# A transformer's selected tokens: moved by rank through a table in memory, in place of one-hot products on TensorE

## The chip, the cores and the metric

The kernel runs on one core of a Trainium2 chip. The metric is the device time of one execution in microseconds (us); the time before is the median of three runs. A profile is one further execution, recorded by the hardware profiler.

The engines are named as in the profile: PE (TensorE, matrix products; PEld is its loading of weights), DVE (VectorE), ACT (ScalarE), POOL (GpSimd) and SP (SyncE, which only issues transfers here). Each engine works through its own instructions in a fixed order and waits at an instruction until the semaphores it needs have come. Transfers between the memories (DMAs) are issued by SP, ACT or POOL and carried out by 16 DMA engines, which all three share.

## The reference

A Fourier neural operator turns 64 images of 256 x 256 into 256 rows of 256 numbers each; 77 rows of text are joined to them, which makes 333 tokens per sample. Then comes one transformer layer. What matters here is its second half, in which only 165 of the 333 tokens are processed:

```python
def ffn(x, wr, br, w1, b1, w2, b2):          # x: normalized tokens, (64, 333, 256)
    weights = (x @ wr + br)[..., 0]          # one weight per token
    k = 333 // 2                             # 166
    _, idx = top_k(weights, k)
    sel_idx = idx[:, :k - 1]                 # the 165 tokens of largest weight
    sel = take_along_axis(x, sel_idx[:, :, None], axis=1)
    h = gelu(sel @ w1 + b1)                  # 256 -> 1024
    y = h @ w2 + b2                          # 1024 -> 256
    y = y * take_along_axis(weights, sel_idx, axis=1)[..., None]
    processed = zeros_like(x).at[batch_idx, sel_idx].set(y)
    return processed + x

h = concatenate([fno(x), txt], axis=1)
h = h + attention(layernorm(h))
h = h + ffn(layernorm(h))
```

## The kernel before

The first 9,800 us, about, compute the Fourier operator over all 64 samples; nothing of that is touched. The last stage, here called the transformer stage, handles one sample after another. A sample's tokens lie in a tile of 128 partitions by three blocks of 256 numbers: two blocks of 128 image rows and one of 77 text rows (`rows = [128, 128, 77]`).

The stage's functions are these. `image_rows(b)` loads sample `b`'s field in eight pieces of 1 MB, `ch`, on SP's queue and contracts them on PE (L896) into the image rows `h`. `attention(h)` normalizes (`layer_norm`, name "a"), forms the attention's products on PE, has POOL add the output bias to `h` (L1020), and on DVE adds the attended values to that (L1027), which gives `h1`; a second `layer_norm` (name "f") gives `z`, the tokens of the feed-forward part.

`select(z)` computes each token's weight as a column (L940), spreads it over all partitions with a diagonal matrix `dg` (L944) and a product with ones (L945), and counts for every token on DVE how many tokens have a larger weight: `gt` (L958 to L963) is the token's rank from 0 to 332. `fw` is the weight where the rank is below KEPT = 165 and zero elsewhere (L964). `place` (L965) is a one-hot matrix of tokens by ranks, made by comparing the rank with a row of numbers from a table, `iota`.

`feed_forward(b, ...)` multiplies `z` by `place` on PE (L1042), which yields the selected tokens already transposed, `zs`; transposes `place` on PE into `back` (L1053); runs the two layers (L1059, L1070), each over 165 columns; transposes the result into `ys` (L1080), ranks on partitions; multiplies it by `back` (L1089), which puts every rank's row at its token and zeros elsewhere; and finally multiplies by `fw` and adds `h1 + z` on DVE (L1092, with the sum from POOL, L1085). Seventeen DMAs from POOL's queue store the sample's rows (L1097, L1101). `evict` copies a result from PE's accumulators (PSUM), on DVE and ACT in turn.

The main loop interleaves samples: it emits the image rows of sample b + 2, the attention of b + 1, the feed-forward of b, and the selection for b + 1. No order is written out by hand in this stage: a scheduler orders each engine's instructions, and a pool's number of buffers (`bufs`, two for most tiles here, six for PSUM) bounds how far samples may overlap. DMAs issued by POOL use eight semaphores in turn, so a DMA waits for the eighth before it to have landed.

Of the kernel before, what the change touches and what calls it, by code (L numbers as in the profile page):

```python
# [8 lines left out]

F32 = mybir.dt.float32  # L10
AF = mybir.ActivationFunctionType
ALU = mybir.AluOpType
AX = mybir.AxisListType
# [9 lines left out]
TOK = S + TXT  # L23
# [11 lines left out]
def _tables():  # L35

    y = np.arange(S)
    ky = np.arange(M)
    kx = np.concatenate([np.arange(M), np.arange(-M, 0)])
    th = 2 * np.pi * np.outer(y, ky) / S  # L40
    tx = 2 * np.pi * np.outer(y, kx) / S
    grid = np.linspace(0.0, 1.0, S, dtype=np.float32)
    p = np.arange(128)
    out = {}

    def halves(a):
        return a.reshape(2, 128, -1).transpose(1, 0, 2)

    def ravel(*dims):

        return np.unravel_index(np.arange(np.prod(dims)), dims)


    fy = np.zeros((S, 32))
    fy[:, :M], fy[:, M:KX] = np.cos(th), -np.sin(th)
    out["fyt"] = np.tile(fy.reshape(8, 32, 32).transpose(1, 0, 2), (4, 1, 1))
    ex = np.zeros((128, S))
    ex[:KX], ex[KX:2 * KX] = np.cos(tx).T, np.sin(tx).T
# [36 lines left out]
    m6 = np.zeros((128, 3, 2, 4, C))  # L95
    for g in range(3):
        for r in range(2):
            for k4 in range(4):
                m6[M * r + 4 * g + k4 + 32 * np.arange(4), g, r, k4] = 1
    out["m6"] = m6  # L100
    out["mk4"] = p[:, None] % 4 == np.arange(128)[None, :] // C

    g = grid.astype(np.float64)
    one = np.ones(S)
    gh = np.zeros((128, 3, 2, KX))
    for j, (a, b) in enumerate(((g, one), (one, g), (one, one))):
        m = np.outer(np.exp(-1j * tx).T @ a, np.exp(-1j * th).T @ b)
        for k4 in range(4):
            gh[4 * j + k4] = np.stack([m.real, m.imag])[:, :, k4::4].transpose(2, 0, 1)
    out["gh"] = gh  # L110

    t, g, n, hc = ravel(2, 4, 4, 8)
    x_of = 64 * n + 16 * g + 2 * hc + t
    out["exT"] = ex[:, x_of]
    out["mask4"] = p[:, None] // C == np.arange(4)[None, :]
    tok = np.concatenate([x_of, S + np.arange(TXT)])
    rows = np.stack([x_of[:128], x_of[128:], S + p], 1)
    out["iota"] = np.repeat(np.arange(KEPT)[None, :], 128, 0)
    out["tri"] = tok[None, None, :] < rows[:, :, None]
    out = {k: np.ascontiguousarray(v.reshape(128, -1), np.float32) for k, v in out.items()}  # L120

    mv = np.zeros((4, 32, 16, S), np.float32)
    mv[:, :KX] = t32[None, :KX, None, :]
    mv[:, 28] = grid
    return out, mv.reshape(128, 16 * S)
# [10 lines left out]
def tile_fno_fusion_transformer(ctx: ExitStack, tc: tile.TileContext, a, cst_d, grid_d, out):  # L136
    nc = tc.nc
# [640 lines left out]
    tcon = ctx.enter_context(tc.tile_pool(name="tcon", bufs=1))  # L778
    inp = ctx.enter_context(tc.tile_pool(name="inp", bufs=7))
    tabt = tables(tcon, "exT", "tri", "cstt")  # L780
    EXT, MASK4, IOTA = tabt("exT"), tabt("mask4"), tabt("iota")
    TRI = tabt("tri").rearrange("p (t j) -> p t j", t=3)
    qrow = tcon.tile([128, C, 1], F32, name="qrow")
    nc.vector.tensor_mul(qrow[:, :, 0], qR, s_)
# [12 lines left out]
    D = S  # L797
# [70 lines left out]
    pb_ = ctx.enter_context(tc.tile_pool(name="tpb", bufs=2, space=PSUM))  # L868
    pp = ctx.enter_context(tc.tile_pool(name="tpp", bufs=6, space=PSUM))

    def psum():
        return pp.tile([128, 512], F32, name="pp")

    def image_rows(b):
        am = ap_.tile([2 * KX, 32 * C], F32, name="am")
# [53 lines left out]
            evict(zT[:, dh, :], ps[:, :TOK], 2)  # L929
        return z, zT  # L930

    def select(z):


        wcol = small.tile([128, 3], F32, name="wcol")
# [10 lines left out]
        wrow = tp.tile([128, TOK], F32, name="wrow")  # L946
        nc.vector.tensor_scalar(wrow, ps[:, :TOK], brB, None, ALU.add)
        fw = small.tile([128, 3], F32, name="fw")
        place = tp.tile([128, 3, KEPT], F32, name="place")
        for t in range(3):  # L950
            r = rows[t]
            junk = tp.tile([128, TOK], F32, name="junk", bufs=1)
            wc = small.tile([128, 1], F32, name="wc")
            nc.vector.scalar_tensor_tensor(
                junk[:r, :r], wrow[:r, toks[t]], 1.0, ID[:r, :r], ALU.mult, ALU.mult, accum_out=wc[:r]
            )
            gt = small.tile([128, 1], F32, name="gt")
            nc.vector.tensor_scalar(junk[:r], wrow[:r], wc[:r], None, ALU.is_gt, ALU.add, accum_out=gt[:r])  # L958
            eq = small.tile([128, 1], F32, name="eq")
            nc.vector.scalar_tensor_tensor(  # L960
                junk[:r], wrow[:r], wc[:r], TRI[:r, t, :], ALU.is_equal, ALU.mult, accum_out=eq[:r]
            )
            nc.vector.tensor_add(gt[:r], gt[:r], eq[:r])  # L963
            nc.vector.tensor_scalar(fw[:r, t:t + 1], gt[:r], float(KEPT), wc[:r], ALU.is_lt, ALU.mult)  # L964
            nc.vector.tensor_scalar(place[:r, t, :], IOTA[:r], gt[:r], None, ALU.is_equal)  # L965
        return fw, place

    def attention(h):
        z, zT = layer_norm(h, "a")
# [41 lines left out]
        for jt in range(3):  # L1011
# [2 lines left out]
            for t in range(3):  # L1014
                nc.tensor.transpose(ps[:r, toks[t]], p_[:rows[t], t, toks[jt]], ID[:rows[t], :rows[t]])
            evict(pT[:r, jt, :], ps[:r, :TOK], 2)
        h1 = tp.tile([128, 3, D], F32, name="h1")
        for t in range(3):
            r = rows[t]
            nc.gpsimd.tensor_add(h[:r, t, :], h[:r, t, :], boB[:r])  # L1020
# [9 lines left out]
        z = layer_norm(h1, "f")  # L1030
        return h1, z

    kept = [slice(0, (KEPT + 1) // 2), slice((KEPT + 1) // 2, KEPT)]

    def feed_forward(b, h1, z, fw, place):

        zs = tp.tile([128, 2, KEPT], F32, name="zs")
        for dh in range(2):
            ps = psum()
            for t in range(3):  # L1040
                r = rows[t]
                nc.tensor.matmul(  # L1042
                    ps[:, :KEPT], lhsT=z[:r, t, 128 * dh:128 * dh + 128], rhs=place[:r, t, :],
                    start=t == 0, stop=t == 2,
                )
            evict(zs[:, dh, :], ps[:, :KEPT], 2)
        back = tp.tile([128, 2, TOK], F32, name="back")
        for c, k in enumerate(kept):
            n = k.stop - k.start
            ps = psum()  # L1050
            for t in range(3):
                r = rows[t]
                nc.tensor.transpose(ps[:n, toks[t]], place[:r, t, k], ID[:r, :r])  # L1053
            evict(back[:n, c, :], ps[:n, :TOK], 2)
        g = tp.tile([128, HID // 128, KEPT], F32, name="g", bufs=1)
        for hb in range(HID // 128):
            ps = psum()
# [18 lines left out]
        for c, k in enumerate(kept):  # L1076
            n = k.stop - k.start
            ps = psum()
            for dh in range(2):
                nc.tensor.transpose(ps[:n, 128 * dh:128 * dh + 128], yT[:, dh, k], ID)  # L1080
            evict(ys[:n, c, :], ps[:n, :D], 2)
        o = tp.tile([128, 3, D], F32, name="o")
        for t in range(3):
            r = rows[t]
            nc.gpsimd.tensor_add(h1[:r, t, :], h1[:r, t, :], z[:r, t, :])  # L1085
            ps = psum()
            for c, k in enumerate(kept):
                n = k.stop - k.start
                nc.tensor.matmul(  # L1089
                    ps[:r, :D], lhsT=back[:n, c, toks[t]], rhs=ys[:n, c, :], start=c == 0, stop=c == 1  # L1090
                )
            nc.vector.scalar_tensor_tensor(  # L1092
                o[:r, t, :], ps[:r, :D], fw[:r, t:t + 1], h1[:r, t, :], ALU.mult, ALU.add
            )
        for g in range(4):
            for n in range(4):
# [5 lines left out]

    hs = {n: image_rows(n) for n in range(min(2, B))}
    done = attention(hs.pop(0))
    done += select(done[1])
    for b in range(B):
        now = done
        if b + 2 < B:
            hs[b + 2] = image_rows(b + 2)
        if b + 1 < B:  # L1110
            done = attention(hs.pop(b + 1))
        feed_forward(b, *now)
        if b + 1 < B:
            done += select(done[1])


# [31 lines left out]
```

## Time and profile before

| | us |
|---|---|
| median of 3 runs | 12,356.92 (12,355.53 to 12,375.24) |
| the profiled execution's own time | 12,360.58 |
| its span, first to last instruction | 12,358.8 |
| from 10,000 to 12,000 us: samples in it | 50 |
| L1059 and L1070 (feed-forward products) in these 2,000 us, PE busy | 234.8 and 231.0 |
| L896 (image rows), PE busy | 364.1 |
| L1042, L1053, L1089 (one-hot products), PE busy | 92.7, 37.0, 143.4 |
| L1097 (output stores), POOL busy | 394.0 |

The page gives each engine's busy share in 40 slices of 309 us; a digit is a tenth, 9 stands for 90% and more, and PEclk is the clock that PE was granted. The view of groups gives busy time by line, operation and shape. The view of windows adds up each engine's busy time in a stretch. The timeline lists an engine's instructions in order of time, with the idle time before one in brackets and what ended it. A landing time is the time from a DMA's issue until its data are reported complete.

### The profile page before, as it was taken

Reading aid. Unit: us, or ns where it says so; the run is one execution under the profiler, and the core shown is the slowest. Engines: PE = TensorE matmul, PEld = TensorE weight load, DVE = VectorE, ACT = ScalarE, POOL = GpSimd, SP = SyncE. Lnnn points to the kernel's source line nnn. Section 1 sums busy time; section 2 is a strip of 40 time slices with the busy share of each in tenths; the row PEclk is TensorE's granted clock in tenths of the full one; section 3 lists DMA queues with packets and bytes.
Section 4 is the critical chain, followed back from the end, with each engine's and each line's share of the span. In section 5 each row is a group of like instructions: output and inputs, shape, how many; then the busy total and the mean of one; then the engine's idle time right before and its main releaser. Section 6 shows DMA issues by size and latency. Waiting matters only on the chain. (4 is left out here: it accounts for less than half of the span.)

```text
span 12358.8 us, 405064 instructions
## 1 busy us (share of the span) xinstructions
PE 11164.5 (90%) x182038; PEld 5874.0 (48%) x182038; DVE 8774.8 (71%) x10667; ACT 6094.5 (49%) x10249; POOL 1412.7 (11%) x1987
## 2 busy tenths in 40 slices
PE   6999999998799999999979999999999699999999
PEld 3444444443444444444434444444444366666666
DVE  6777777777776777777766777767777566666665
ACT  5555555555555555555544555555555333333333
POOL 0000000000000000000010000000000133333333
PEclk8999999999899999999989999999999799999999
DMA  7555555555899999888889989889899755555554
GB/s 226 200 199 203 203 201 201 201 200 210 325 354 349 349 351 350 348 347 348 346 302 352 354 346 355 339 339 353 346 351 352 247 234 227 219 228 233 218 223 152
DMA packets 589283, 3485.06 MB, mean 282 GB/s; under 512 B 95000, under 2 KB 144536, under 8 KB 188568
## 3 DMA queue, kind: packets, MB, share of 16 engines
q1 hardware_dynamic: 539520, 3392.84, 71.2%
q0 software_dynamic: 40880, 62.59, 2.0%
q8 instruction: 1423, 23.31, 0.8%
q10 hardware_dynamic: 7144, 3.72, 0.1%
q14 instruction: 316, 2.59, 0.1%
HBM read 1761.87 MB, written 1696.92 MB: 280 GB/s over the span
## 5 line engine op out<-in xcount | busy, mean ns | idle before, releaser
L666 ACT ACTIVATE ring<-ring 128x1024 f32<-128x1024 f32 x3072 | 3108.8, 1012 | 1186.4 <-PE ring L659 1148.7
L647 DVE STREAM_TRANSPOSE t<-vo 128x2048 f32<-128x2048 f32 x1536 | 3550.0, 2311 | 175.1 <-ACT vo L642 14.5
L659 PE MATMUL ring<-vo,w 32*32 32x512 f32 x49152 | 2849.3, 622 | 392.2 <-DVE zt L686 138.7
L642 ACT ACTIVATE vo<-ring 128x1024 f32<-128x1024 f32 x1536 | 1568.2, 1021 | 2997.7 <-PE ring L635 2378.9
L643 DVE TENSOR_SCALAR vo<-ring 128x1024 f32<-128x1024 f32 x1536 | 1857.7, 1209 | 608.2 <-PE ring L635 420.4
L676 PE MATMUL ring<-t,cst 32*32 32x512 f32 x49152 | 1864.7, 601 | 303.7 <-issue 302.1
L686 DVE STREAM_TRANSPOSE zt<-ring 128x1024 f32<-128x1024 f32 x384 | 711.8, 1925 | 1658.6 <-PE ring L676 1658.6
L659 PEld LDWEIGHTS ring<-vo,w 32*32 32x32 f32 x49152 | 761.3, 105 | 1898.7 <-ACT ring L666 477.0
L676 PEld LDWEIGHTS ring<-t,cst 32*32 32x32 f32 x49152 | 975.9, 103 | 1157.0 <-issue 707.8
L594 POOL TENSOR_TENSOR ams<-am,sk 48x512 f32<-48x512 f32 x384 | 486.9, 1268 | 8642.4 <-DMA am<-mix 8039.9
L635 PE MATMUL ring<-vin,ws 32*32 32x512 f32 x32768 | 1238.0, 606 | 22.1 <-issue 19.8
L699 PEld LDWEIGHTS ring<-cst,zt 128*128 128x128 f32 x4608 | 536.4, 194 | 174.6 <-ACT vo L642 161.6
L666 ACT ACTIVATION_READ_ACCUMULATOR ring<-ring 128x1 f32 x3072 | 584.1, 190 | 0.0
L1097 POOL DMA_DIRECT2D out_dram<-o x1024 | 504.4, 501 | 659.8 <-DVE o L1092 628.2
L699 PE MATMUL ring<-cst,zt 128*128 128x96 f32 x4608 | 568.7, 281 | 8.1 <-DVE zt L686 8.1
L896 PE MATMUL hp<-ch,win 128*32 128x512 f32 x4096 | 472.0, 601 | 8.3 <-DMA ch<-v 8.1
L635 PEld LDWEIGHTS ring<-vin,ws 32*32 32x32 f32 x32768 | 253.5, 103 | 407.9 <-issue 377.8
L605 PE MATMUL ring<-ams,cst 49*128 49x512 f32 (+1 forms) x1536 | 391.5, 621 | 37.6 <-POOL ams L594 27.2
L901 ACT ACTIVATE h<-hp,hbias 128x512 f32<-128x512 f32 x64 | 44.0, 687 | 595.5 <-PE hp L896 595.5
L419 PE MATMUL mps<-wm,xh 32*64 32x128 f32 (+1 forms) x4608 | 121.3, 374 | 203.4 <-ACT e L431 74.1
L1059 PE MATMUL pp<-zs,w 128*128 128x165 f32 x2048 | 302.1, 305 | 0.0
L1070 PE MATMUL pp<-g,w 128*128 128x165 f32 x2048 | 298.6, 303 | 0.0
(936 smaller groups left out, 11812.8 us busy)
## 6 DMA issues: line engine op xcount, KB each, us to landing
v<-vo SPq DMA_DIRECT2D x1536, 1024.0 KB
vin<-v SPq DMA_DIRECT2D x1024, 1024.0 KB
ch<-v SPq DMA_DIRECT2D x512, 1024.0 KB
mix<-ob SPq DMA_DIRECT2D x96, 512.0 KB
am<-mix SPq DMA_DIRECT2D x384, 96.0 KB
xin<-in_x_dram SPq DMA_DIRECT2D x16, 1024.0 KB
mv<-in_x_dram SPq DMA_DIRECT2D x256, 64.0 KB
out_dram<-o POOLq DMA_DIRECT2D x1024, 16.0 KB, 3.0
```

The source lines that it names most:

```text
L594: nc.gpsimd.tensor_tensor(ams[b % 2][hv], a_[hv], sk[hv].rearrange("p c k -> p (c k)"), ALU.mult)
L635: nc.tensor.matmul(ps[n][32 * j:32 * j + 32], lhsT=ws[32 * n:32 * n + 32], rhs=v[32 * n:32 * n + 32, 2 * j:2 * j + 2, :], start=False, sto ...
L642: nc.scalar.activation(of[:, 0:2], t2[0], AF.Relu)
L643: nc.vector.tensor_scalar(of[:, 2:4], t2[1], 0.0, None, ALU.max)
L647: nc.vector.transpose(t32[b, t // 2][:, :, 8 * (t % 2):8 * (t % 2) + 8, :].rearrange("p y s c -> p s y c"), o.rearrange("p s (y l) -> p s ...
L659: nc.tensor.matmul(ps[n][32 * j:32 * j + 32], lhsT=w4[i + 1][32 * n:32 * n + 32], rhs=o[32 * n:32 * n + 32, 2 * j:2 * j + 2, :], start=Tru ...
L666: nc.scalar.activation(t2[n], t2[n], AF.Square, accum_out=acc[:, at:at + 1])
L676: nc.tensor.matmul(ps[n][32 * j:32 * j + 32], lhsT=FYT[32 * n:32 * n + 32, k, :], rhs=t32[b, j][32 * n:32 * n + 32, k].rearrange("p s c -> ...
L686: nc.vector.transpose(zt[:, h].rearrange("p k c -> p c k"), t2[h].rearrange("p n (s c) -> p c (n s)", c=C),)
L699: nc.tensor.matmul(ps[:, 0, 96 * g:96 * g + 96], lhsT=zt[:, h, k0:k0 + 4, :].rearrange("p k c -> p (k c)"), rhs=FX[:, h, 48 * r:48 * r + 9 ...
L896: nc.tensor.matmul(hp[32 * g:32 * g + 32], lhsT=win[:, 7 - t:39 - t], rhs=ch[:, g], start=False, stop=t == 7, skip_group_check=True,)
L1097: nc.gpsimd.dma_start(out[b, 64 * n + 16 * g:64 * n + 16 * g + 16].rearrange("(p t) d -> p t d", t=2), o[32 * g + 8 * n:32 * g + 8 * n + 8 ...
```

## The change

The rank, until now compared with a row of numbers to make a one-hot matrix, is turned into an index. In `select`, each block of tokens is written by an indirect DMA, row by row, to its rank's row in a table in the chip's memory (`z_d`, 333 rows of 256 numbers; the name of the tile is `zr` with a number), and the first 165 rows are read back as `zr`, in two DMAs of 83 and 82 rows. In `feed_forward`, four transposes on PE turn `zr` into `zs`. The result `ys` is written to a second table (`y_d`, 166 rows, the last one zero, written once at the start), and an indirect DMA reads for every token the row of its rank, or the zero row where its rank is 165 or more (`idx[..., 1]`, the minimum of rank and 165). The last multiply-add and the stores move to a function `finish`, emitted one iteration later than before, after the next attention. There are three tables of either kind, used in turn, `h1` has three buffers in place of two, and the table `iota` goes.

```diff
+    z_d = [dram.tile([TOK, D], F32, name=f"zr{n}") for n in range(3)]
+    y_d = [dram.tile([KEPT + 1, D], F32, name=f"yr{n}") for n in range(3)]
+    zero = tcon.tile([1, D], F32, name="zero")
+    nc.vector.memset(zero, 0.0)
+    for q in y_d:
+        nc.gpsimd.dma_start(q[KEPT:KEPT + 1], zero)
...
-    def select(z):
+    def select(b, z):
...
-        place = tp.tile([128, 3, KEPT], F32, name="place")
+        idx = small.tile([128, 3, 2], U32, name="idx")
...
-            nc.vector.tensor_scalar(place[:r, t, :], IOTA[:r], gt[:r], None, ALU.is_equal)
-        return fw, place
+            nc.vector.tensor_copy(idx[:r, t, 0:1], gt[:r])
+            nc.vector.tensor_scalar(idx[:r, t, 1:2], gt[:r], float(KEPT), None, ALU.min)
+            nc.gpsimd.indirect_dma_start(
+                z_d[b % 3][:, :], bass.IndirectOffsetOnAxis(ap=idx[:r, t, 0:1], axis=0), z[:r, t, :], None
+            )
+        zr = tp.tile([128, 2, D], F32, name="zr")
+        for c, k in enumerate(kept):
+            nc.gpsimd.dma_start(zr[:k.stop - k.start, c, :], z_d[b % 3][k])
+        return fw, idx, zr
...
-        h1 = tp.tile([128, 3, D], F32, name="h1")
+        h1 = tp.tile([128, 3, D], F32, name="h1", bufs=3)
...
-    def feed_forward(b, h1, z, fw, place):
+    def feed_forward(b, h1, z, fw, idx, zr):
 
         zs = tp.tile([128, 2, KEPT], F32, name="zs")
-        for dh in range(2):
-            ps = psum()
-            for t in range(3):
-                r = rows[t]
-                nc.tensor.matmul(
-                    ps[:, :KEPT], lhsT=z[:r, t, 128 * dh:128 * dh + 128], rhs=place[:r, t, :],
-                    start=t == 0, stop=t == 2,
-                )
-            evict(zs[:, dh, :], ps[:, :KEPT], 2)
-        back = tp.tile([128, 2, TOK], F32, name="back")
+        ps = psum()
         for c, k in enumerate(kept):
             n = k.stop - k.start
-            ps = psum()
-            for t in range(3):
-                r = rows[t]
-                nc.tensor.transpose(ps[:n, toks[t]], place[:r, t, k], ID[:r, :r])
-            evict(back[:n, c, :], ps[:n, :TOK], 2)
+            for dh in range(2):
+                nc.tensor.transpose(
+                    ps[:, KEPT * dh + k.start:KEPT * dh + k.stop], zr[:n, c, 128 * dh:128 * dh + 128], ID[:n, :n]
+                )
+        evict(zs.rearrange("p h k -> p (h k)"), ps[:, :2 * KEPT], 2)
...
+        for c, k in enumerate(kept):
+            nc.gpsimd.dma_start(y_d[b % 3][k], ys[:k.stop - k.start, c, :])
         o = tp.tile([128, 3, D], F32, name="o")
         for t in range(3):
             r = rows[t]
+            nc.gpsimd.indirect_dma_start(
+                o[:r, t, :], None, y_d[b % 3][:, :], bass.IndirectOffsetOnAxis(ap=idx[:r, t, 1:2], axis=0)
+            )
             nc.gpsimd.tensor_add(h1[:r, t, :], h1[:r, t, :], z[:r, t, :])
-            ps = psum()
-            for c, k in enumerate(kept):
-                n = k.stop - k.start
-                nc.tensor.matmul(
-                    ps[:r, :D], lhsT=back[:n, c, toks[t]], rhs=ys[:n, c, :], start=c == 0, stop=c == 1
-                )
+        return o, h1, fw
+
+    def finish(b, o, h1, fw):
+        for t in range(3):
+            r = rows[t]
             nc.vector.scalar_tensor_tensor(
-                o[:r, t, :], ps[:r, :D], fw[:r, t:t + 1], h1[:r, t, :], ALU.mult, ALU.add
+                o[:r, t, :], o[:r, t, :], fw[:r, t:t + 1], h1[:r, t, :], ALU.mult, ALU.add
             )
...
     done = attention(hs.pop(0))
-    done += select(done[1])
+    done += select(0, done[1])
+    last = None
     for b in range(B):
         now = done
         if b + 2 < B:
             hs[b + 2] = image_rows(b + 2)
         if b + 1 < B:
             done = attention(hs.pop(b + 1))
-        feed_forward(b, *now)
+        if last:
+            finish(b - 1, *last)
+        last = feed_forward(b, *now)
         if b + 1 < B:
-            done += select(done[1])
+            done += select(b + 1, done[1])
+    finish(B - 1, *last)
```

More of the change, by code (lines that the diff above doesn't have):

```diff
@@ L10 @@
 F32 = mybir.dt.float32
+U32 = mybir.dt.uint32
 AF = mybir.ActivationFunctionType
@@ L117, in _tables @@
     rows = np.stack([x_of[:128], x_of[128:], S + p], 1)
-    out["iota"] = np.repeat(np.arange(KEPT)[None, :], 128, 0)
     out["tri"] = tok[None, None, :] < rows[:, :, None]
@@ L780, in tile_fno_fusion_transformer @@
     tabt = tables(tcon, "exT", "tri", "cstt")
-    EXT, MASK4, IOTA = tabt("exT"), tabt("mask4"), tabt("iota")
+    EXT, MASK4 = tabt("exT"), tabt("mask4")
     TRI = tabt("tri").rearrange("p (t j) -> p t j", t=3)
@@ L869, in tile_fno_fusion_transformer @@
     pp = ctx.enter_context(tc.tile_pool(name="tpp", bufs=6, space=PSUM))
+    kept = [slice(0, (KEPT + 1) // 2), slice((KEPT + 1) // 2, KEPT)]
     def psum():
         return pp.tile([128, 512], F32, name="pp")
+    z_d = [dram.tile([TOK, D], F32, name=f"zr{n}") for n in range(3)]
[4 more added lines that the diff above has]
+        nc.gpsimd.dma_start(q[KEPT:KEPT + 1], zero)
     def image_rows(b):
@@ L1031, in attention @@
         return h1, z
-    kept = [slice(0, (KEPT + 1) // 2), slice((KEPT + 1) // 2, KEPT)]
-    def feed_forward(b, h1, z, fw, place):
+    def feed_forward(b, h1, z, fw, idx, zr):
         zs = tp.tile([128, 2, KEPT], F32, name="zs")
-        for dh in range(2):
-            ps = psum()
-            for t in range(3):
-                r = rows[t]
-                nc.tensor.matmul(
-                    ps[:, :KEPT], lhsT=z[:r, t, 128 * dh:128 * dh + 128], rhs=place[:r, t, :],
-                    start=t == 0, stop=t == 2,
-                )
-            evict(zs[:, dh, :], ps[:, :KEPT], 2)
-        back = tp.tile([128, 2, TOK], F32, name="back")
+        ps = psum()
         for c, k in enumerate(kept):
             n = k.stop - k.start
-            ps = psum()
-            for t in range(3):
-                r = rows[t]
-                nc.tensor.transpose(ps[:n, toks[t]], place[:r, t, k], ID[:r, :r])
-            evict(back[:n, c, :], ps[:n, :TOK], 2)
+            for dh in range(2):
[3 more added lines that the diff above has]
+        evict(zs.rearrange("p h k -> p (h k)"), ps[:, :2 * KEPT], 2)
         g = tp.tile([128, HID // 128, KEPT], F32, name="g", bufs=1)
```

## The prediction, written before the changed kernel ran

> **What bounds the kernel now.** I read the page's slices first, to find the stage that the change touches, then a table of windows over one period of it, then the timeline of each engine over the same period, then the landing times of POOL's DMAs. The change lies in the transformer stage alone: the last eight slices of the page (from about 9,800 us), in which each of 64 samples is one period.
>
> ```profile
> PE   6999999998799999999979999999999699999999
> DVE  6777777777776777777766777767777566666665
> POOL 0000000000000000000010000000000133333333
> PEclk8999999999899999999989999999999799999999
> ```
>
> ```profile
> core 0: us, PE busy (x) PEld busy (x) DVE busy (x) ACT busy (x) POOL busy (x), PEclk, DMA share, GB/s
> 11005.00:11009.00 4.00, 4.00 (x30) 2.31 (x32) 3.50 (x6) 0.44 (x1) 3.85 (x8) 1.00 0.15 25
> 11009.00:11031.00 22.00, 21.81 (x132) 12.66 (x122) 17.64 (x75) 8.55 (x16) 6.71 (x13) 1.00 0.98 392
> 11031.00:11042.00 11.00, 10.56 (x76) 10.04 (x75) 4.79 (x15) 5.97 (x15) 2.52 (x3) 1.00 0.08 27
> ```
>
> PE is busy for 39.1 of the 40.0 us of a period (the four windows from 11,002 to 11,042 summed), at full clock: PE bounds the stage. To be seen as well: the DMA engines are full (0.98) for 22 us of each period, while the eight 1 MB loads `ch` of a later sample run, and nearly idle for the other 18.
>
> ```profile
> 11001.41 0.45 PE L1080 MATMUL pp<-cst,yT 128*83 128x128 f32 x2 [0.27 <-ACT yT L1074]
> 11002.26 2.87 PE L1089 MATMUL pp<-ys,back 83*128 83x256 f32 x12 [0.41 <-DVE ys L178]
> 11004.97 0.61 PE L945 MATMUL pp<-dg,cst 128*128 128x128 f32 x4
> ...
> 11029.43 1.85 PE L1042 MATMUL pp<-place,fz 128*128 128x165 f32 x12
> 11031.12 0.74 PE L1053 MATMUL pp<-cst,place 128*83 128x128 f32 x6
> 11031.70 4.70 PE L1059 MATMUL pp<-zs,w 128*128 128x165 f32 x32
> ```
>
> The columns are start, length, engine, line. L1080 recurs at 11,041.38: a period is 40.0 us. L1042 and L1053 fill 11,029.43 to 11,031.70; L1089 and the wait before it fill 11,001.86 to 11,004.97.
>
> ```profile
> 11005.15 7.86 POOL L1097 DMA_DIRECT2D out_dram<-o  x16 [9.83 <-DVE o L1092]
> 11013.00 0.53 POOL L1101 DMA_DIRECT2D out_dram<-o  x1
> 11021.70 2.18 POOL L1020 TENSOR_TENSOR h<-h,boB 128x256 f32<-128x256 f32 x3 [8.17 <-DVE az L918]
> 11032.78 2.52 POOL L1085 TENSOR_TENSOR h<-h,fz 128x256 f32<-128x256 f32 x3 [8.90 <-DVE fz L918]
> ```
>
> POOL works 13.1 us of 40 and waits for data the rest; nothing on PE waits for it today. The landing times of its stores, from the view of one line in a window: 1.7 to 1.8 us for the first two L1097 after 11,005 (DMA engines nearly idle), 1.8 us median in the last 18 us of the kernel (no loads left), but a median of 3.1 us and up to 8.0 us for L1097 over 10,000 to 12,000 us, and 5.3 to 8.6 us for L1101, the last of each 17.
>
> **What the Trainium skill says.** "DMA: Bandwidth & Descriptors", section "Anatomy of one DMA", puts the fixed cost of a GpSimd DMA at about 2.0 us; the trace agrees where the engines are idle (1.7 to 1.8). Its section "Queues, rings and completion order" says that a DMA engine takes turns between queues a packet at a time; so under the `ch` load every small packet waits for a large one, which fits the 3 to 8 us. Its section "Two DMAs through the same engine are not ordered" says that a DMA that reads what another wrote must wait for that one's completion; the changed kernel's program has these waits. No page prices the issue of an indirect DMA.
>
> **The change on PE, per period.** Removed: L1042 and L1053, 31.70 - 29.43 = 2.27 us, and L1089 with its wait, 3.11 us. Added: four transposes of `zr` (two L1080 took 0.38 to 0.45 us, so about 0.6 until four are through) and one eviction of 330 columns that nothing hides, since the first feed-forward product (today L1059) needs the whole of it and is next in PE's order (0.49 us by the 333-column DVE copies): 1.1 us. Before, L1053 stood behind the eviction of `zs`. PE's own period: 40.0 - 2.27 - 3.11 + 1.1 = 35.7 us.
>
> **On DVE and ACT.** `place` goes (three at 0.29 to 0.31 us) and two small index instructions per tile come (about 0.15 each by the 128x1 rows): nothing. The two evictions of `back` go. DVE has 27.1 us of work per period; it bounds nothing.
>
> **On POOL.** The order of the changed kernel's instructions shows, per period: two stores of `ys`; three gathers, the first waiting for both stores to land; scatter 1; scatter 2, waiting for scatter 1 to land (both write the same table); three output stores; scatter 3, waiting for scatter 2; three more stores; two reads of `zr`, waiting for scatter 3; the other 11 output stores; then the three adds of L1020 (L1037 in the changed file), which the attention's residual on DVE needs; then the three adds of L1085, and round again. POOL stands still in each of these waits, and everything behind stands too. In DVE's order the three final multiply-adds, which wait for the gathers to land, stand before the third tile's index; so scatter 3 comes after the gathers have landed in any case.
>
> Prices. A direct DMA: 0.50 us of POOL (0.53 for 77 rows). An indirect DMA of 128 rows isn't in the trace. Lower bound 0.54 us, what the POOL issue of `xh` (128 rows, direct, L758) took. For the upper one I take 2.5 us, twice the 1.27 us of the slowest frequent POOL instruction, the 48x512 product of L594: software that handles 128 indices one by one may cost that. I choose 1.2, near that instruction. Landing after the issue is done: 1.3 us idle (1.8 - 0.5); under load 2.6, which is between that and the 4.5 us (5.0 - 0.5) that stores with a backlog show.
>
> The sum, from the moment at which PE starts L945 (0; its order and that of the attention are otherwise kept). `ys` is evicted at 0.4; stores issued to 1.4; landed at 3.3, since the load starts only at 4. Gathers 3.3 to 6.9. Index 1 is ready at 5.9 (today the first `gt`, L963, is ready 5.6 us after L945, plus two small ones), so scatter 1 goes at 6.9 and, with the gathers' packets before it (0.7), lands at 11.4. Scatter 2 lands at 15.2, scatter 3 at 19.0: each 1.2 + 2.6. Reads of `zr` issued to 20.0 and landed by 23. PE wants them at 24.5 (29.43 - 4.97): hidden, with 1.5 us to spare. The 11 stores run to 25.5, some 0.5 more for the wait on the eighth DMA before, first add done at 26.9. Today it is done 17.5 after L945 and its user starts at 22.1, so this one is late by 5. From the residual (11,027.1) to the second `dg` (11,035.9) DVE takes 8.8 us: `dg` at 35.7. PE asks for it at 34.8, 0.9 before its period's end. So the period becomes 36.6 to 36.7: PE is no longer the bound, but the loop stores, gathers, scatters, reads, stores, add, layer norm, `dg` is, by 1 us.
>
> Against the profiled execution's own 12,360.6 us (span 12,358.8): 63 x (40.0 - 36.7) = 208 us less. At the end a tail grows: the last sample's multiply-adds wait for a store, three gathers and their landing, about 9 us where L1089 took 3: 6 us more. 12,360.6 - 208 + 6 = 12,159; the median of the three runs is 3.7 us lower, so 12,155 us.
>
> **Rivals.** (1) PE stays the bound: if an indirect DMA takes below about 1.0 us or lands 0.4 us sooner under load, the loop closes within 35.7: 12,360.6 - 63 x 4.3 + 6 - 4 = 12,092. For it: the direct issue is nearly flat in rows (0.50 to 0.54). Against: the software must read indices, and scatters run in the full 22 us. (2) The loop decides, and is longer than today's period: the slower side. Six indirect issues stand in it one after another (three gathers, three scatters), so each 0.1 us more costs 0.6 per period; from 1.75 us on (3.3 / 6 above 1.2), or 1.1 us more for each loaded landing, the period passes 40. At 2.5 us the chain becomes: gathers to 10.8, scatters to 26.1, reads 27.1, stores 33, add 33.8, `dg` 42.6, period 43.5: 12,360.6 + 63 x 3.5 + 2 = 12,583. For it: three serial round trips under a full DMA load, and 8 us landings seen. Against: those 8 us have 16 stores queued ahead. (3) The reads of `zr` come late at PE and set the end before `dg` does: with landings 3 us later than in my sum, the transposes start 1.5 us late and the period is 35.7 + 1.5 = 37.2, so 12,155 + 63 x 0.5 = 12,187. For it: a margin of only 1.5 us; against: by then most of the load has passed.
>
> **Chances.** PE remains the bound (12,080 to 12,110): 0.25. The loop at 36.2 to 39.5 us (12,115 to 12,330), rival 3 in it: 0.40. Within 0.2% (25 us, about what a measurement of this kernel tells from no change): 0.05. Slower: 0.30, half of it up to 12,480. So faster 0.65, same 0.05, slower 0.30. The range 12,085 to 12,480 leaves out the worse half of the slow case, and the fastest few in a hundred; the likeliest case's own range is 12,115 to 12,330.
>
> **What would show it.** The period in PE's timeline (36.7; 35.7 if PE bounds). The mean of an indirect DMA on POOL: 1.2. Waits of POOL's scatters on a DMA of about 2.6 each, and about 1 us of PE idle before L945 (L955 in the changed file), released by `dg`; no idle before the transposes of `zr`. If PE waits for `zr` first, or POOL never delays the residual's add, my order of the limits is wrong; an indirect DMA above 1.75 us turns the sign.

## The result, and the profile after

The changed kernel takes 12,831.36 us (median of four runs, 12,823.83 to 12,834.28) against 12,357.02 us (four runs, 12,355.53 to 12,375.24): a ratio of 1.038, with a 95% interval of 1.0361 to 1.0397. It is slower by 474 us, where 202 us less were predicted, and outside the stated range of 12,085 to 12,480. Its profiled execution took 12,829.99 us, with a span of 12,828.1.

First the page's slices of the changed kernel, 321 us each; the transformer stage fills the last nine or so.

```profile
PE   6999999997999999999789999999996888888877
POOL 0000000001000000000100000000002444444445
PEclk8999999998999999999899999999997888888888
DMA  7555555556999989898888989888887555655564
```

Nothing differs up to the stage. In it PE is at 7 to 8 tenths instead of 9, and the clock it was granted is at 8 tenths instead of 9: PE has become an engine that waits, and in part it works at a lower clock. The windows over one period say the same with numbers, cut at the start and the end of the `ch` loads.

```profile
core 0: us, PE busy (x) PEld busy (x) DVE busy (x) ACT busy (x) POOL busy (x), PEclk, DMA share, GB/s
11000.00:11004.00 4.00, 4.00 (x33) 1.71 (x35) 3.64 (x9) 0.21 (x1) 0.61 (x2) 1.00 0.24 62
11004.00:11026.00 22.00, 17.66 (x90) 9.51 (x83) 12.96 (x65) 7.16 (x14) 7.75 (x9) 0.90 1.01 375
11026.00:11034.00 8.00, 4.87 (x18) 3.35 (x16) 3.27 (x9) 0.00 (x0) 4.28 (x10) 0.85 0.44 165
11034.00:11047.00 13.00, 12.36 (x76) 12.07 (x76) 6.24 (x15) 7.22 (x15) 9.03 (x14) 0.87 0.09 19
```

The full load (1.01) lasts 22 us, as before; in it PE is busy for 17.7 us where it was for 21.8. PE's timeline shows where it stands (start, length, line, and in brackets the idle time before and what ended it).

```profile
10998.09 0.61 PE L955 MATMUL pp<-dg,cst 128*128 128x128 f32 x4
...
11021.80 2.53 PE L1032 MATMUL pp<-cst,prob 128*128 128x128 f32 x9 [3.28 <-ACT prob L1010]
11024.41 6.12 PE L1041 MATMUL pp<-v,probT 128*128 128x256 f32 x18
11033.62 0.34 PE L1057 MATMUL pp<-cst,zr 83*128 83x83 f32 x2 [3.09 <-DMA zr<-zr]
...
11035.01 6.43 PE L1065 MATMUL pp<-zs,w 128*128 128x165 f32 x32 [0.53 <-ACT zs L176]
...
11046.00 0.61 PE L955 MATMUL pp<-dg,cst 128*128 128x128 f32 x4
```

This period is 47.9 us long. PE waits for the selected rows `zr` (3.09 us before the transposes L1057) and, earlier, for the attention's exponentials (3.28 us before L1032); the 32 products L1065 then take 6.43 us, where the same products took 4.70 before. It does not wait for `dg` at L955, the place where I had it wait. Over 1,500 us, 31.5 periods, the view of waits gives:

```profile
PE pp L1057 <- DMA zr<-zr: 129.4, 45, 6.2
DVE o L1102 <- DMA o<-yr,idx: 127.5, 73, 5.8
POOL zr L982 <- DMA zr<-fz,idx: 79.0, 24, 4.6
PE pp L1003 <- ACT qT L995: 74.0, 20, 5.3
```

(us in all, times, the longest.) So PE loses 4.1 us per sample to `zr` and 2.3 to `qT`, an input of the attention's first product. POOL's timeline over the same period shows why `zr` is late:

```profile
10999.56 1.04 POOL L1089 DMA_DIRECT2D yr<-ys  x2 [4.14 <-ACT ys L176]
11004.46 1.04 POOL L1093 DMA_INDIRECT o<-yr,idx  x1 [3.85 <-issue]
11005.80 1.03 POOL L1093 DMA_INDIRECT o<-yr,idx  x1 [0.30 <-issue]
11007.14 0.97 POOL L1093 DMA_INDIRECT o<-yr,idx  x1 [0.30 <-issue]
11008.42 1.01 POOL L977 DMA_INDIRECT zr<-fz,idx  x1 [0.30 <-issue]
11018.27 0.98 POOL L977 DMA_INDIRECT zr<-fz,idx  x1 [8.83 <-DVE am L888]
11019.26 1.70 POOL L1107 DMA_DIRECT2D out_dram<-o  x3
11025.00 1.03 POOL L977 DMA_INDIRECT zr<-fz,idx  x1 [4.04 <-DVE sm L1026]
...
11031.32 1.06 POOL L982 DMA_DIRECT2D zr<-zr  x2 [3.72 <-DMA zr<-fz,idx]
```

Each indirect DMA costs POOL 1.0 us; the rest is waiting. From one scatter's issue to the next 9.85 and 6.73 us pass, and 6.32 to the reads L982. The DVE lines named beside scatters 2 and 3 are the last semaphore events that the profile saw and have no data for them; by the program, what scatter 2 waits for is the landing of scatter 1 (both write the same table), and for scatter 3 that of scatter 2. The trace's semaphore records, which hold sixteen reports for each of these DMAs (the last is taken as its landing), agree: the scatters land at 11,017.50, 11,024.15 and 11,030.78, and POOL's next step comes 0.77, 0.85 and 0.54 us after each; over 41 periods these three gaps hardly change (medians 0.77, 0.88 and 0.54). Last, DVE's and ACT's timelines:

```profile
11012.24 0.48 DVE L1102 SCALAR_TENSOR_TENSOR o<-o,fw,h 128x256 f32<-128x256 f32 x1 [5.53 <-DMA o<-yr,idx]
...
11014.81 0.48 DVE L1102 SCALAR_TENSOR_TENSOR o<-o,fw,h 128x256 f32<-128x256 f32 x1 [1.61 <-DMA o<-yr,idx]
...
11016.35 0.48 DVE L1102 SCALAR_TENSOR_TENSOR o<-o,fw,h 77x256 f32<-77x256 f32 x1 [0.99 <-DMA o<-yr,idx]
...
11019.19 0.29 DVE L921 BATCH_NORM_AGGREGATE amv<-abs 128x2 f32<-128x6 f32 x2
```

```profile
11019.51 0.30 ACT L923 ACTIVATE ars<-amv,epsc 128x3 f32<-128x3 f32 x1 [5.09 <-DVE amv L921]
11019.82 1.28 ACT L1010 ACT_TABLE_LOAD   x1
11021.12 0.54 ACT L1010 ACTIVATE prob<-pp,mx 128x333 f32<-128x333 f32 x1
```

DVE stands for 8.1 us in the three final multiply-adds, until the gathers of `y` have landed. Behind them in its order stand the statistics of a later sample's layer norm (L921), ready near 11,019.5. ACT stands 5.09 us waiting for these at L923 and so comes to the exponentials L1010 only at 11,021.12, and PE waits for the exponentials at L1032.

### The profile page after: what moved, and what is told of

It is laid out like the page before. It is cut to its first block, busy times and chain, and to the rows that moved or that the text cites. A ratio compares the mean times of both kernels' runs of the same rounds, so it can differ in the third digit from the quotient of the medians.

```text
span 12828.1 us, 402887 instructions
## 1 busy us (share of the span) xinstructions
PE 11133.3 (87%) x180374; PEld 5816.3 (45%) x180374; DVE 8790.4 (69%) x10764; ACT 6072.0 (47%) x10153; POOL 1983.2 (15%) x2630
## 5 line engine op out<-in xcount | busy, mean ns | idle before, releaser
L1107 POOL DMA_DIRECT2D out_dram<-o x1024 | 532.7, 527 | 41.9 <-issue 17.8
L1065 PE MATMUL pp<-zs,w 128*128 128x165 f32 x2048 | 420.1, 380 | 36.6 <-DVE zs L178 19.8
L1065 PEld LDWEIGHTS pp<-zs,w 128*128 128x128 f32 x2048 | 404.1, 252 | 51.4 <-DVE zs L178 27.5
L1003 PE MATMUL pp<-azT,qT 128*128 128x333 f32 (+1 forms) x768 | 279.7, 514 | 150.2 <-ACT qT L995 150.0
L1102 DVE SCALAR_TENSOR_TENSOR o<-o,fw,h 128x256 f32<-128x256 f32 (+1 forms) x192 | 92.7, 483 | 423.2 <-DMA o<-yr,idx 265.4
```

Of the source, the lines that this page charges most:

```text
L1065: nc.tensor.matmul(ps[:, :KEPT], lhsT=w1[:, dh, 128 * hb:128 * hb + 128], rhs=zs[:, dh, :], start=dh == 0, stop=dh == 1,)
L1107: nc.gpsimd.dma_start(out[b, 64 * n + 16 * g:64 * n + 16 * g + 16].rearrange("(p t) d -> p t d", t=2), o[32 * g + 8 * n:32 * g + 8 * n + 8 ...
```

## The experiments

My theory after the result: the indirect DMAs are cheap to issue, but under the `ch` load each lands late, and two engines that work in order, POOL and DVE, stand in these landings. The rivals: the time lies in POOL's software for each indirect DMA, whatever the load; or only one of the two engines matters. Single runs are compared with runs of the kernel before made beside them, which are given; these lie between 12,344 and 12,394 us, so differences below some 50 us are not read. As a second measure I counted samples in 10,000 to 12,000 us of each trace (its first feed-forward products divided by 32): 50 before, 42 after.

**Without the load.** Seven of the eight loads of a sample fall away; POOL's instructions keep the order that they have in the changed kernel. The same edit was made in the kernel before, as a control.

```diff
-            ch = inp.tile([128, 4, 2, S], F32, name="ch")
-            nc.sync.dma_start(ch.rearrange("p g r y -> p (g r) y"), src[b][:, t])
+            if t == 0:
+                ch = inp.tile([128, 4, 2, S], F32, name="ch")
+                nc.sync.dma_start(ch.rearrange("p g r y -> p (g r) y"), src[b][:, t])
```

> The changed kernel, with only the first of a sample's eight 1 MB pieces ch loaded and contracted eight times (seven eighths of the image data are left out; PE's work is the same). Theory A, the small DMAs land late because the ch loads fill the DMA engines: landings fall to about 3.5 us, the chain stores, gathers, scatters, reads closes before PE needs zr, and the period falls from 47.3 to 35.7 to 36.7 us, the time to 12,090 to 12,190 us. Theory B, each indirect DMA costs POOL's software about 2.5 us whatever else runs: the period stays above 45, the time above 12,650 us.

> The kernel before with the same seven eighths of the image loads left out, as a control. Both theories: PE bounds its stage, so the time stays within 30 us of 12,357 us. If it falls by more, what the lighter loads give the changed kernel is not due to landings alone.

Measured: 12,076.32 us for the changed kernel and 12,330.08 for the control, beside 12,394.42. The control gains 64 us from light loads; the changed kernel drops by 755 us below its own median and has 56 samples in the 2,000 us. From the timeline of POOL in this kernel, one period:

```profile
11000.60 1.21 POOL L978 DMA_INDIRECT zr<-fz,idx  x1 [0.30 <-DVE o L1103]
11004.08 0.98 POOL L978 DMA_INDIRECT zr<-fz,idx  x1 [2.26 <-DVE am L888]
...
11007.65 1.03 POOL L978 DMA_INDIRECT zr<-fz,idx  x1 [0.96 <-DVE mx L1009]
...
11010.75 1.06 POOL L983 DMA_DIRECT2D zr<-zr  x2 [0.51 <-PE pp L1018]
```

The steps are 3.5, 3.6 and 3.1 us, in place of 9.85, 6.73 and 6.32, at the same issue cost. So POOL's software isn't the loss; the landing under load is. And with landings a little shorter than I had assumed, the changed kernel is 254 us faster than the control: the gain on PE is real.

**Scatters that do not wait for each other.** The ranks of a sample differ, so its three scatters never write one row twice; a declaration takes the waits between them away.

```diff
+        scat = []
...
-            nc.gpsimd.indirect_dma_start(
+            scat.append(nc.gpsimd.indirect_dma_start(
                 z_d[b % 3][:, :], bass.IndirectOffsetOnAxis(ap=idx[:r, t, 0:1], axis=0), z[:r, t, :], None
-            )
+            ))
+            for q in scat[:-1]:
+                tc.declare_no_dep(scat[-1].ins, q.ins, reason="ranks differ")
```

> The changed kernel with the three scatters of a sample not waiting for one another (their ranks differ, so their rows don't meet); all else stays. Theory S, the three landings one after another are the largest part of the loop: scatter 2 is issued right after scatter 1, scatter 3 only waits for its index behind the gathers' landing, zr comes 6 to 9 us earlier, and the time falls to 12,250 to 12,450 us. Theory P, the order on POOL and DVE (the third index behind the gathers) sets the end: the scatters' waits move to the index, and the time stays above 12,650 us.

Measured: 12,553.48 us (12,394.42 beside it), 47 samples: between the two expectations. Without the serial waits the time is 278 us below that of the changed kernel (315, when each is counted against the kernel before beside it), but what is left is still slower than before. Scatter 3 still comes after the gathers' landing, since its index stands behind the multiply-adds on DVE, and PE still waits for `qT`, 5.2 us in the period looked at.

**One half of the change at a time.** In the first kernel only `y` goes through its table, and `z` is selected by one-hot products as before; in the second it is the other way round. The second was made from the kernel before, not from the changed one: it has no `finish`, so its multiply-adds and stores stay in `feed_forward`, and `back` has one buffer in place of two.

```diff
 # y only, in select and feed_forward
-            nc.vector.tensor_copy(idx[:r, t, 0:1], gt[:r])
...
-            nc.gpsimd.indirect_dma_start(
-                z_d[b % 3][:, :], bass.IndirectOffsetOnAxis(ap=idx[:r, t, 0:1], axis=0), z[:r, t, :], None
-            )
...
+            nc.vector.tensor_scalar(place[:r, t, :], IOTA[:r], gt[:r], None, ALU.is_equal)
...
+                nc.tensor.matmul(
+                    ps[:, :KEPT], lhsT=z[:r, t, 128 * dh:128 * dh + 128], rhs=place[:r, t, :],
+                    start=t == 0, stop=t == 2,
+                )
...
```

> Half of the change: the selected rows come from the one-hot product on PE as before, the results go back by table and gather. Theory S: without scatters the loop is short, PE bounds at about 36.5 us with at most 2 us of stalls behind the gathers on DVE: 12,130 to 12,300 us, faster than before. Theory G, the gathers' landings (8 us each under load, with DVE standing in them) cost as much as the scatters: above 12,500 us.

> The other half of the change: rows selected by scatter and read back, results placed by the one-hot product on PE as before. Without gathers and without stores of ys, DVE never stands in a DMA. PE alone would need 38.8 us. If the three scatters one after another (6.5 us each under the load) decide, zr lands about 28 us after the ranks' start where PE asks at 24.5, the period is 42 to 44 and the time 12,480 to 12,700 us. If the cost of the changed kernel lay in the gathers alone, as in the run with only that half, PE bounds and the time is 12,260 to 12,320 us.

Measured: 12,660.24 us for `y` alone (12,394.42 beside it, 45 samples) and 12,968.46 us for `z` alone (12,361.23 beside it, 40 samples). Each of these two kernels is slower than the kernel before; since the second has the old order of multiply-adds and stores, the two losses are not the halves of the whole. For `y` alone there is no scatter and no `zr`, and PE's timeline in a period reads:

```profile
11047.93 2.59 PE L998 MATMUL pp<-azT,qT 128*128 128x333 f32 x4 [6.20 <-ACT qT L990]
```

In DVE's, the first multiply-add before that waits 5.50 us and the second 1.90 us for the gathers; ACT, ahead of `qT` in its order, stands 6.78 us for the layer norm's statistics behind them. The second kernel missed its expectation, and is slower even than the whole change. POOL's timeline there shows its place: the sixteen stores of L1108 stand in POOL's order ahead of scatter 1, and with eight in flight they and the last one take from 10,999.9 to 11,014.5 under the load. Scatter 1 goes at 11,015.17, the reads at 11,031.45, and PE waits for `zr`:

```profile
11033.78 1.09 PE L1054 MATMUL pp<-cst,zr 83*128 83x83 f32 x4 [9.57 <-DMA zr<-zr]
```

I had not counted the stores ahead of it.

**The final multiply-adds later on DVE.** They are placed after the next sample's attention residual (L1044), where their data have long landed: alone on the whole change, on the kernel with `y` alone, and on the whole change with free scatters.

```diff
         if last:
-            finish(b - 1, *last)
+            with tc.issue_after(mark[0].ins):
+                finish(b - 1, *last)
```

(`mark[0]` is the last instruction of L1044.)

> The changed kernel with one order changed: the final multiply-adds of a sample come on DVE behind the residual of the next attention, by which time the gathers have landed. Theory D, DVE standing in the gathers' landing holds up ACT and PE, and the third index: that standing goes, but scatters still wait for one another: period about 43, 12,480 to 12,650 us. Theory S alone, only the scatters' round trips matter: no better than 12,750 us.

> Only the results by table (no scatters), with the final multiply-adds late on DVE. Theory D: nothing on PE's path waits for a DMA from POOL any more; PE bounds at 36.4 us: 12,110 to 12,200 us, faster than both kernels. If the gathers cost in another way (POOL standing before them delays the residual's add, or POOL's stores delay it), the time stays above 12,300 us.

> The changed kernel with both edits: late multiply-adds, and scatters that don't wait for one another. The six indirect DMAs share the DMA engines with the ch loads, some 2.5 us each per 128 rows, so zr lands 3 to 4 us after PE asks: period 39 to 41, 12,300 to 12,430 us. If only the waits and not the shared engines cost: PE bounds at 35.7, 12,090 to 12,130 us.

Measured, all beside 12,361.23 us: 12,848.17 for the whole change, a miss; 12,143.22 for `y` alone, as expected; 12,601.72 for the last, a miss. For `y` alone this one move is worth 517 us (from 12,660; 484, when each is counted against the kernel before beside it), so there DVE's standing was the loss. Its gathers land 8.1 to 8.6 us after their issue in the period shown, about as in the other kernels under the load, and nothing waits for them; PE's idle time in a period is 0.39 and 0.77 us:

```profile
11032.81 4.25 PE L1038 MATMUL pp<-v,probT 128*128 128x256 f32 x18 [0.39 <-ACT probT L177]
11036.90 1.85 PE L1054 MATMUL pp<-place,fz 128*128 128x165 f32 x12
11039.52 4.75 PE L1063 MATMUL pp<-zs,w 128*128 128x165 f32 x32 [0.77 <-DVE zs L179]
```

In the whole change the same move brings nothing, since the loss moves into another wait. PE's timeline has, in the place of the waits for `qT`:

```profile
11035.84 0.78 PE L1059 MATMUL pp<-cst,zr 83*128 83x83 f32 x4 [9.55 <-DMA zr<-zr]
```

The scheduler now put the gathers between scatters 1 and 2, so that the scatters go at 11,009.31, 11,016.26 and 11,024.84 and the reads at 11,031.34. In the kernel with both edits the gathers stand there as well: the scatters no longer wait for each other, but two of them come behind three gathers that nothing needs yet, and the reads stand 7.72 us until the last of the six has landed.

**Shorter packets in the loads.** The prediction had every small packet wait for a large one of the loads. If so, small transfers would come through sooner when the packets of the loads are shorter. `ch` is padded, so that each of its transfers goes in pieces of 2 KB; the data are the same. (In a window of 100 us the load queue has 20.0 MB in 10,096 packets, in place of 17.4 MB in 2,627.)

```diff
-            ch = inp.tile([128, 4, 2, S], F32, name="ch")
-            nc.sync.dma_start(ch.rearrange("p g r y -> p (g r) y"), src[b][:, t])
+            ch = inp.tile([128, 4, 2 * S + 8], F32, name="ch")
+            nc.sync.dma_start(ch[:, :, 0:2 * S], src[b][:, t].rearrange("p (g r) y -> p g (r y)", r=2))
...
```

> The changed kernel with the ch loads cut into pieces of 2 KB per partition row in place of 8 KB (the tile's groups are padded by 8 numbers, so a row of 8 KB is no longer one run); same bytes, same PE work. Theory A1, small DMAs wait their turn behind one large packet at a time: a quarter of the packet's size brings landings from 6 to 8 us down to 4 to 5 us, and the time falls to 12,350 to 12,550 us. Theory A2, they wait behind a fixed amount of bytes already queued, or the write itself is slow under load: no change, 12,780 to 12,880 us.

Measured: 12,815.21 us (12,353.17 beside it, median of nine), 42 samples. The landings hardly moved: by the semaphore records from 10,050 to 12,000 us the gathers land 7.8 us after their issue (median), in place of 8.5 in the changed kernel, and the scatters 6.1 in place of 6.4. So the size of the loads' packets, as the profile counts them, doesn't set the lateness. Whether the unit in which a DMA engine takes turns became smaller with them, no run shows.

**An order for both.** If only the standing counts, the order decides: the three scatters right after the stores of `ys`, without waits between them; then the reads of `zr`; only then the gathers; and the multiply-adds after the next sample's second layer norm.

```diff
+            mark[1] = nc.gpsimd.dma_start(zr[:k.stop - k.start, c, :], z_d[b % 3][k])
...
         if last:
-            finish(b - 1, *last)
+            with tc.issue_after(mark[0].ins):
+                finish(b - 1, *last)
         last = feed_forward(b, *now)
         if b + 1 < B:
             done += select(b + 1, done[1])
+        with tc.issue_after(mark[1].ins):
+            last = gather(b, *last)
```

(`gather` holds the three gathers and POOL's adds of `h1` and `z`, taken out of `feed_forward`; `mark[0]` is here the last instruction that writes `z`. The free scatters of the second experiment are in it too.)

> The whole change with POOL's order made for it: scatters that don't wait for one another come right behind the stores of ys, then the reads of zr, and only then the gathers; the final multiply-adds come on DVE behind the next sample's second norm, so their stores come last. If the loop of waits was all that cost, scatters go 6 to 10 us after the ranks' start, zr lands at 22 to 24 us, PE asks at 24.5: PE bounds at 35.7, 12,080 to 12,150 us. If three scatters and two reads under the load need more than that by themselves, PE waits for zr and its clock falls: above 12,200 us.

> The kernel with only the results by table and late multiply-adds once more, timed: PE bounds, 12,125 to 12,160 us, 1.6 to 1.9 per cent less than before.

Measured beside 12,353.17 us (nine runs, 12,344.26 to 12,388.58): 12,126.71 us with this order (four runs, 12,109.02 to 12,145.73), a ratio of 0.981 (0.9794 to 0.9832); and 12,141.71 us for `y` alone with late multiply-adds (five runs, 12,128.11 to 12,146.53), a ratio of 0.982 (0.9807 to 0.9836). Both are faster than the kernel before, by 1.9 and 1.8 per cent, and than the changed one; which of the two is faster the intervals don't tell. POOL's timeline of the ordered kernel:

```profile
11043.48 1.05 POOL L1094 DMA_DIRECT2D yr<-ys  x2
11048.30 1.08 POOL L980 DMA_INDIRECT zr<-fz,idx  x1 [3.77 <-DVE idx L979]
11049.98 1.00 POOL L980 DMA_INDIRECT zr<-fz,idx  x1 [0.60 <-DVE idx L979]
11051.64 0.97 POOL L980 DMA_INDIRECT zr<-fz,idx  x1 [0.66 <-DVE idx L979]
11057.84 1.12 POOL L987 DMA_DIRECT2D zr<-zr  x2 [5.23 <-PE pp L1008]
11059.27 1.03 POOL L1101 DMA_INDIRECT o<-yr,idx  x1 [0.30 <-issue]
```

One landing of scatters stands in the path of `zr`, in place of three one after another, and it starts 4.8 us after the stores of `ys` were issued, as soon as the indices are there. The PE line named beside L987 is again only a last semaphore event: the three scatters land at 11,055.19, 11,056.47 and 11,057.30, and the reads go 0.5 us after the last. Over the 1,500 us PE waits 8.5 us for `zr`, in place of 129.4. The scatters land after 6.3 to 6.6 us (medians of three windows), still under the full load. Against the kernel with both edits (12,601.72) two things differ, the gathers' place and that of the multiply-adds; the 475 us between them are not split.

## Why the prediction was wrong, by its own steps

The loop, from the start of L955, as predicted and in the period shown:

| step | predicted, us | measured, us |
|---|---|---|
| first store of `ys` issued | 0.4 | 1.5 |
| gathers begin | 3.3 | 6.4 |
| scatter 1 | 6.9 | 10.3 |
| scatter 2 | 11.4 | 20.2 |
| scatter 3 | 15.2 | 26.9 |
| reads of `zr` issued | 19.0 | 33.2 |
| PE has `zr` | by 23 | 35.5 |
| first add of L1037 done | 26.9 | 40.8 |
| next L955 | 36.7 | 47.9 |

- **The step that failed: "landing ... under load 2.6" after the issue is done.** The three scatters of this period landed 8.1, 4.9 and 4.8 us behind their issue, where the sum has 3.3 (2.6, and 0.7 for the gathers' packets), 2.6 and 2.6: 9.2 us more. Between a landing and POOL's next step 0.8, 0.9 and 0.5 us more pass, which the sum put at nothing; the issues took 0.2 less each. That makes the scatters' three steps 10.8 us longer (22.9 against 4.5, 3.8 and 3.8). Of the 12.5 us by which `zr` is late (35.5 against 23), the second large part is the first gather, which went 3.9 us after the issue of the stores of `ys` was done, where 1.9 was set. That part belongs to the period shown: the median of 40 periods is 2.3, with the light loads as well. The smaller differences (1.1 and 0.4 more before the scatters, 1.7 less for the reads) nearly cancel. Rival 2 had the break-even at "1.1 us more for each loaded landing"; the measured excess was about three times that.
- **Where the 2.6 came from.** The better figure stood in the trace before. In the period that the prediction shows, the eight stores issued up to 11,008.60 landed after 1.7 to 1.9 us, and the eight from 11,009.58 on, with the load, after 5.2 to 6.8, which is 4.7 to 6.3 behind their issue. The median of 3.1 mixes the two, and the "5.0" of "stores with a backlog" is in no view on record. A backlog of sixteen was not the reason: the first of the late ones, which took 5.2, had three stores still under way.
- **"Hidden, with 1.5 us to spare": wrong by the same term.** `zr` closes the loop. From its arrival to the next L955 are 12.4 us (11,033.62 to 11,046.00), and 35.5 + 12.4 is the period. Rival 3 named the right wait; its landings were too short.
- **The bound by `dg`: a path that is not there.** PE waits for `dg` nowhere. The sum has POOL's add of the output bias, done at 26.9, hold up the residual at 22.1. But that add belongs to a later sample. In the kernel before, the add at 11,021.70 is for the residual at 11,067.07, and the one at 11,027.10 has had its add for 45 us; in the changed kernel a sample's residual comes 37 us after its add (median of 64), and in the period shown it stands before POOL's adds:

```profile
11027.44 0.48 DVE L1044 SCALAR_TENSOR_TENSOR h<-pp,sm,h 128x256 f32<-128x256 f32 x1 [2.26 <-PE pp L1041]
11038.04 2.59 POOL L1037 TENSOR_TENSOR h<-h,boB 128x256 f32<-128x256 f32 x3
```

Both signs that the prediction named for a wrong order of the limits came true: PE waits for `zr`, and POOL does not delay the residual's add. With every other term as it was set, PE would have bounded the period at 35.7 us. So a landing of the right size in the same sum would have given the right sign, but its period of 36.7 rested on a wait that doesn't exist.
- **"It bounds nothing" of DVE: wrong.** I saw that the multiply-adds stand before the third index, and counted for scatter 3 alone. Everything behind them in DVE's order stands as well, layer norm and softmax among it, and through ACT that reaches PE. With `y` alone it costs 517 us.
- **PE's own period of 35.7 us: right as work.** In the ordered kernel PE is busy for 1,421.88 us of the 1,500 from 10,500 on, at clock 1.00, which at its mean period of 36.1 us (from 10,064.07 to 11,977.54 there are 53) is 34.2 per sample. In the changed kernel it is busy for 1,224.54 of the same stretch, at a mean clock of 0.89; with the mean period of 47.6 us (from 10,045.57 to 11,997.80 there are 41) that is 38.9 per sample for the same products. So its period is 34.2 of work at full clock, 4.7 more that go with the lower clock (34.2 / 0.89 is 38.4), and 8.7 of standing. That the clock would fall with the waits was not in my sum.
- **An indirect DMA of 1.2 us on POOL: right, a little high** (means of 1.02 for scatters and 1.09 for gathers). The order of POOL's instructions, which the sum followed, was right too.
- **The sign.** The chance of 0.30 for slower was put on rival 2, whose worked case is a dear issue (2.5 us; its chain leaves out the 0.7 us for the gathers' packets, and is 44.2 with it). Its mechanism, a loop longer than the period before, is what happened, through the landing and not the issue. Sixty-three periods that are longer by 47.6 - 40.0 make 479 us, against 469 between the profiled executions (12,829.99 - 12,360.58); the last ones, which have no loads beside them, are shorter (the last two stores of `ys` are 30.0 us apart).

## What to carry to other kernels

In this kernel an indirect DMA's price was its landing under the load at that moment, and that counted once for each instruction of an in-order engine that stood in it. Measure it there, apart from the landings without load; a median over both hid it here. What decided was then order: chain no landings that needn't be chained, issue what is needed first first, and put whoever reads the result behind everything else that its engine has to do. One of two such moves alone may bring nothing, because the next wait takes its place: late multiply-adds gained nothing in the whole change (12,848 us) and 517 us with `y` alone.

## What the runs showed of the hardware

- The issue of an indirect DMA takes POOL 1.0 to 1.2 us (means of the kernels) for up to 128 rows, with the load and without. Its landing, counted from the issue's start (medians of windows of 100 us): 2.7 to 4.4 us with light loads, 7.7 to 8.4 with free scatters, 6.3 to 7.1 in the ordered kernel, 7.7 to 9.1 for gathers with `y` alone and late multiply-adds. Direct transfers are late in the same way: 1.7 to 1.9 us without the load and 5.2 to 6.8 with it for the stores of one period of the kernel before.
- Under the load even the first packet is late: the record of packets has the gather of 11,004.46 begin at 11,008.67, 4.2 us after its issue; the one at 12,809.04, when the loads are over, begins at 12,810.78, 1.7 us after. Scatter 2 (11,018.27) begins at 11,022.44, 4.2 us after. I had put this down to small packets waiting for large ones; with loads in 2 KB pieces a gather's first packet still comes 4.4 us after its issue (median, as in the changed kernel). What holds them up stays open.
- PE's granted clock goes with its idle time. After 3.1 us of idle the 32 products L1065 take 6.43 us at a granted clock of 0.76 (window 11,034.5 to 11,041.5); after 0.77 us, in the kernel with `y` alone and late multiply-adds, they take 4.75. "TensorE: Matmul & The Clock Gate" of the Trainium skill, section "HAM oscillation — how this bites in real kernels", gives as its rule no gaps above about 3.4 us; here somewhat less was enough, and so it was in a period of the ordered kernel with waits of 1.84 and 0.93 us a third of a us apart (6.43 us). That the idle time is the cause is the page's account; the runs show only that the two go together.
